# Diagonal products in four pieces, and another order of the node tiles, in a two-layer graph attention kernel

## The chip, the cores and the metric

The kernel runs on one core of a Trainium2 chip. The metric is the device time of one execution in microseconds (us); the time of a kernel is the median of its runs.

## The reference

The input is a graph with 10000 nodes of 768 float32 features and 170000 directed edges (`src`, `dst`, sorted by `dst`, one self-loop for each node). The reference adds a self-loop to every node again, which the kernel does by counting a node's own loop twice. What is computed, cut to what matters:

```python
def gat_conv(x, edge_index, W, a_src, a_dst, bias, heads, out_ch, concat):
    xl = (x @ W).reshape(n, heads, out_ch)
    e = leaky_relu(alpha_src[src] + alpha_dst[dst], 0.2)   # alpha = sum over channels of xl * a
    e = exp(e - segment_max(e, dst)[dst])
    alpha = e / (segment_sum(e, dst)[dst] + 1e-16)
    return segment_sum(xl[src] * alpha, dst) + bias        # 4 heads of 256, then 1 head of 768

h  = relu(layer_norm(gat_conv(x, W1 ...))) + (x @ Wr1 + br1)      # 1024 wide
h2 = layer_norm(gat_conv(h, W2 ...)) + (h @ Wr2 + br2)            # 768 wide
out = layernorm(x + h2)
```

## The kernel before, in words

**Preparation (0 to 888 us).** For each of 79 tiles of 128 nodes TensorE multiplies `x` by `W1` and the rows, with their attention terms, go to `table1` in HBM. Beside it VectorE and GpSimd sort the nodes by falling number of in-edges. From then on tile `t` holds the 128 nodes at places 128t to 128t+127 of that sorting, so tile 0 has the nodes with the most in-edges. The number of *slots* of a tile, the largest number of in-edges that its nodes may have, is fixed when the kernel is built (`slot_counts`): 41 for tile 0, then 27, 26, 25, 24, 24, 23, 23, 22 (four times), 21 (4), 20 (6), 19 (7), 18 (7), 17 (8), 16 (7), 15 (8), 14 (6), 13 (5), 12 (3), 11 (3), 10, 9 and 8; 1377 in all.

**The order of the tiles.** `TURNS` (L111) is the order in which both layers take the tiles. `paired` (L79) takes by turns one from the half with few in-edges and one from the half with many: it begins with 17, 17, 17, 17, 17, 18, 16, 18 slots, spreads to 11, 26, 9, 41, 10, 27, 11 in the middle, comes back to 18, 17, 18, 17, 17, and ends with the tile of 8.

**The ring.** A slot of a tile is one gathered row for each of its 128 nodes, one indirect DMA that GpSimd issues (L437). The rows go into a ring in SBUF, of 29 slots in layer 1 and of 41 in layer 2; slot number q+29 (q+41) is asked for once slot q has been read by all its readers (`Ring.fetch`). In layer 2 the first slot of a tile, its own rows, is a plain load on SyncE's queue (L465).

**Layer 1** (`ordered_layer1`). Each instruction stream is written out in the order of its engine, without a scheduler. For a tile: `weights_of` computes the attention weights `e` of all its slots (`logits`, L484; so all its slots must have landed), and for its first `on_pe(t)` slots (1 for tiles below 14 slots, 2 for 14 and 15, 3 for 16 and 17, 4 from 18) ScalarE writes, for each of the 4 heads, a 128x128 diagonal matrix with the weights (L735), by which TensorE multiplies the head's 256 columns of the gathered rows into the PSUM tile `acc` (`summed`, L741). The remaining slots are added into `acc` by VectorE: three in four have been multiplied by ScalarE (L521) and are added (L528), the fourth is multiplied and added head by head (L532). TensorE's other work for a tile does not depend on the slots: 14 transposes (L711), the product with `Wr1` (L184, 512 columns at a time), and the product with `W2` (L829). Its order is: diagonal products of tile t+1 behind the `W2` product of tile t-1, then the transposes and the `Wr1` product for tile t+1, then the `W2` product of tile t. The tile of 41 slots doesn't fit the ring and is taken in parts (`attend_parts`).

**Layer 2** (`ordered_layer2`). VectorE weighs and adds the first 512 of the 768 columns of every slot (L532). The last 256 columns are TensorE's: ScalarE writes one diagonal matrix for each slot (L939; five tiles of four matrices) and TensorE multiplies (L940) into the PSUM tile that holds the residual. The residual of a tile is `x` by an identity (L951) and `h` by `Wr2` (L954). TensorE takes the residual of tile t+2 after the diagonal products of tile t+1. The normalised rows are scattered to the output by GpSimd (L973).

A float32 product of TensorE appears in the profile as two passes, each a weight load (PEld) and a matmul (PE): 956 matrices of L735 make 1912 matmuls of L741, and 1377 of L939 make 2754 of L940.

Of the kernel before, what the change touches and what calls it, by code (L numbers as in the profile page):

```python
# [33 lines left out]
AX = mybir.AxisListType  # L34

P = 128
BANK = 512
BIG = 1.0e30
SLOPE = 0.2
# [6 lines left out]
G = 4  # L46
# [4 lines left out]
ON_PE2 = 512  # L51
# [4 lines left out]
def chunk_counts(n_edges):  # L56

    used = n_edges // P + 1
    return used, -(-used // P) * P + G


def slot_counts(n_nodes, n_edges):
# [7 lines left out]
    counts = []  # L70
    for t in range(-(-n_nodes // P)):
        room = t * P if t else 0.002
        k = next((k for k, m in enumerate(tails)
# [2 lines left out]
    return counts  # L76


def paired(n):  # L79

    last = n - 1
    half = last // 2
    many = list(range(half - 1, -1, -2))
    many += sorted(set(range(half)) - set(many))
    few = list(range(half, last, 2))
    few += sorted(set(range(half, last)) - set(few), reverse=True)
    turns = []
    for i in range(len(few)):
        turns += few[i:i + 1] + many[i:i + 1]
    return turns + [last]  # L90


@with_exitstack
def gnn_kernel(ctx, tc, x, x_cols, src, dst, src_col, dst_col, W1, a_src1, a_dst1, b1, g1, be1, Wr1, br1,
               W2, a_src2, a_dst2, b2, g2, be2, Wr2, br2, out, n_edges):
    nc = tc.nc
    N, D0 = out.shape
    H1, DH1 = a_src1.shape
    H2, DH2 = a_src2.shape
    C1, C2 = H1 * DH1, H2 * DH2  # L100


    R1, R2 = C1 + 2 * H1 + 1, C2 + 2 * H2
    NT = -(-N // P)
    NP = NT * P
    NCH = src_col.shape[1]
# [1 line left out]
    CAPS = slot_counts(N, n_edges)  # L108
    SLOTS = CAPS

    TURNS = paired(NT)  # L111
    FIRST, TOTAL = [0] * NT, 0
    for t in TURNS:
        FIRST[t], TOTAL = TOTAL, TOTAL + SLOTS[t]
# [50 lines left out]
    def transposed(pool, a, n, name):  # L165

        k = n // P
        aT = pool.tile([P, k, P], F32, name=name)
        for j in range(0, k, BANK // P):
            m = min(BANK // P, k - j)  # L170
            p = ps_tr.tile([P, BANK // P, P], F32, name="tr")
            for i in range(m):
# [4 lines left out]
    def product(aT, w, n, pool=None):  # L177

        k = w.shape[1]
        p = (pool or ps_big).tile([P, 2 * BANK], F32, name="big")  # L180
        for c in range(0, n, BANK):
            e = min(n, c + BANK)
            for j in range(k):
                nc.tensor.matmul(p[:, c:e], aT[:, j, :], w[:, j, c:e], start=(j == 0), stop=(j == k - 1))  # L184
        return p
# [298 lines left out]
    def logits(small, ring, lo, hi, ad, heads, c, top=None):  # L484


        n = hi - lo
        e = small.tile([P, ring.size, heads], F32, name="e")[:, :n]
        for a, b, rows in ring.parts(lo, hi):
            nc.vector.tensor_tensor(e[:, a - lo:b - lo], rows[:, :, c + heads:c + 2 * heads],  # L490
                                    ad[:, None, :].to_broadcast([P, b - a, heads]), op=OP.add)
        leaky(e, e)
        new = small.tile([P, heads], F32, name="new")
        nc.vector.reduce_max(new, e.rearrange("p k h -> p h k"), axis=AX.X)
        if top is not None:
            nc.vector.tensor_max(new, new, top)
        nc.vector.tensor_tensor(e, e, new[:, None, :].to_broadcast([P, n, heads]), op=OP.subtract)
        nc.scalar.activation(e, e, AF.Exp)  # L498
        for a, b, rows in ring.parts(lo, hi):
            if not ring.own:  # L500
                nc.vector.tensor_scalar(slots[:, a:b], rows[:, :, R1 - 1], -1.0, float(NP), op0=OP.mult, op1=OP.min)  # L501
                nc.vector.memset(rows[:, :, c + heads:], -BIG)
        return e, new

    def normalised(small, e, heads, t):

        doubled(e, t)
        total = small.tile([P, heads], F32, name="total")
        nc.vector.reduce_sum(total, e.rearrange("p k h -> p h k"), axis=AX.X)
        nc.vector.tensor_scalar(total, total, 1e-16, None, op0=OP.add)  # L510
        nc.vector.reciprocal(total, total)
        nc.vector.tensor_mul(e, e, total[:, None, :].to_broadcast([P, e.shape[1], heads]))  # L512

    def doubled(e, t):
        nc.vector.tensor_scalar(e[:, 0], e[:, 0], loops[:, TURNS[t]:TURNS[t] + 1], None, op0=OP.mult)

# [60 lines left out]
    def pieces(a, width):  # L577

        return [a[:, c:c + width] for c in range(0, a.shape[1], width)]
# [35 lines left out]
    with tc.tile_pool(name="w1", bufs=1) as w1p, tc.tile_pool(name="l1", bufs=2) as io, \  # L615
# [51 lines left out]
        for t in range(NT):  # L667
# [3 lines left out]
            for i, vec in enumerate((ad_b, as_b)):  # L671
                m = io.tile([P, C1], F32, name="scr")
                nc.vector.tensor_mul(m, p[:, :C1], vec)  # L673
                for h in range(H1):
                    s = slice(h * DH1, (h + 1) * DH1)
# [9 lines left out]

    SLOTS, FIRST = [SLOTS[t] for t in TURNS], [FIRST[t] for t in TURNS]

    def nodes(t):
        return order[:, TURNS[t]:TURNS[t] + 1]

    def ordered_layer1():
        with tc.tile_pool(name="b1", bufs=1) as pool, tc.tile_pool(name="small1", bufs=2) as small, \
# [3 lines left out]
            ring = Ring(pool, table1, R1, RING1, {})  # L696
# [34 lines left out]
            def summed(acc, diagonals, e, q, lo, hi, m):  # L731

                for k in range(lo, hi):
                    for i in range(H1):
                        nc.scalar.activation(diagonals[:, k * H1 + i, :], ident, AF.Copy,  # L735
                                             scale=e[:, k, i:i + 1])
                for k in range(lo, hi):
                    for i in range(H1):

                        c, d = i * DH1, (i + 1) * DH1  # L740
                        nc.tensor.matmul(acc[:, c:d], diagonals[:, k * H1 + i, :], ring.slot(q + k)[:, c:d],  # L741
                                         start=(k == 0 and c % BANK == 0),
                                         stop=(k == m - 1 and (d % BANK == 0 or d == C1)),
                                         skip_group_check=True)

            def weights_of(t):

# [13 lines left out]
            last = None  # L761
# [4 lines left out]
            def store(t):  # L766
# [5 lines left out]
                full = None  # L772
                nc.sync.dma_start(table2[TURNS[t] * P:(TURNS[t] + 1) * P, :], row)

# [5 lines left out]
            for t in range(NT + 1):  # L780
                live, events = t < NT, []
                n = SLOTS[t] if live else 0
# [13 lines left out]
                if whole:  # L796
                    e, acc = ready
# [49 lines left out]
                if live and not whole:  # L847
                    due(n)
                    sums, acc = (ps_acc.tile([P, 2 * BANK], F32, name="acc") for _ in range(2))
# [25 lines left out]
                last = None  # L875
                if live:
                    last = r, acc
            store(NT - 1)

    def ordered_layer2():  # L880
        nonlocal ps_big
        with tc.tile_pool(name="b2", bufs=1) as pool, tc.tile_pool(name="small2", bufs=2) as small, \
# [5 lines left out]
            parts = pieces(w2.rearrange("p k n -> p (k n)")[:, :6 * C1], C1)  # L888
            ring = Ring(pool, table2, R2, RING2, dict(zip(FIRST, TURNS)))

# [34 lines left out]
            def weights_of(t):  # L925


                n = SLOTS[t]
                ad = small.tile([P, H2], F32, name="ad")
                nc.vector.tensor_add(ad, ring.slot(FIRST[t])[:, C2:C2 + H2], lift)  # L930
                e, _ = logits(small, ring, FIRST[t], FIRST[t] + n, ad, H2, C2)
                yield e
                normalised(small, e, H2, t)
                to = rs[t][:, C2:2 * C2 - ON_PE2]
                nc.tensor.matmul(to, ones, b2_b[0:1, ON_PE2:], start=False, stop=False, skip_group_check=True)
                for k in range(n):
                    if k % G == 0:
                        diagonals = pool.tile([P, G, P], F32, name="diagonals", bufs=DIAGONALS)
                    nc.scalar.activation(diagonals[:, k % G, :], ident, AF.Copy, scale=e[:, k, :])  # L939
                    nc.tensor.matmul(to, diagonals[:, k % G, :], ring.slot(FIRST[t] + k)[:, ON_PE2:C2],  # L940
                                     start=False, stop=(k == n - 1), skip_group_check=True)
                yield

            def residual(t):
# [14 lines left out]
            def norms(t, h, r, means):  # L959

                stats = deviation(small, [a for m in means for a in pieces(m, C2 - ON_PE2)])
                yield
                scaled(h, means, stats, g2_b, be2_b)
                nc.vector.tensor_add(h, h, r[:, :C2])
                mean, inv = deviation(small, pieces(h, C2 // 2))
                yield
                nc.vector.reciprocal(inv, inv)
                less = small.tile([P, 1], F32, name="less")
                nc.vector.scalar_tensor_tensor(less, mean, -1.0, inv, op0=OP.mult, op1=OP.mult)
                o = pool.tile([P, C2], F32, name="out")  # L970
                nc.scalar.activation(o, h, AF.Identity, bias=less, scale=inv)
                yield
                nc.gpsimd.indirect_dma_start(  # L973
                    out=out, out_offset=bass.IndirectOffsetOnAxis(ap=nodes(t), axis=0),
                    in_=o, in_offset=None, bounds_check=N - 1, oob_is_err=False)

            assert C2 % BANK and C2 % BANK + C2 - ON_PE2 <= BANK
            q = product(brT, wr2, C2)
            rs = {0: residual(0)}
            last = iter(())  # L980
            ready = []
            assert whole(0)
            for t in range(NT):
                n = SLOTS[t]
# [3 lines left out]
                if not whole(t):  # L988
# [5 lines left out]
                    last = norms(t, h, rs[t], [h])  # L994
                else:
                    e = (ready or list(weights_of(t)))[0]
                    acc = ps_acc.tile([P, BANK], F32, name="acc")
# [24 lines left out]
                    last = norms(t, h, rs[t], [acc, rs[t][:, C2:2 * C2 - ON_PE2]])  # L1022
# [274 lines left out]
```

## Time and profile before

| | |
|---|---|
| median of 3 runs (lowest to highest) | 5709.45 us (5708.44 to 5711.98) |
| the profiled execution's own time | 5708.44 us |
| its span, first to last instruction | 5706.6 us |
| busy: TensorE / VectorE / GpSimd / ScalarE | 4919.0 / 4317.0 / 3222.9 / 3159.9 us |
| preparation, layer 1, layer 2 (first gather into the ring at 887.7, first residual near 3487) | 888, 2599, 2220 us |
| mean granted TensorE clock | 0.92 |

The busy time of TensorE counts a matmul from its start to a modelled end that lies behind the start of the next; the time from one start to the next is what a matmul takes in a stream. In a row of the timeline the first two numbers are the start and the length in us, then engine, line, operation, names, shapes and the number of instructions; in brackets stands the idle time before it and what ended it. "issue" there means that the engine waited for nothing that the profile shows.

### The profile page before, as it was taken

What the parts mean: (1) busy time and instruction counts of PE and PEld (TensorE: products, weight loads), DVE (VectorE), ACT (ScalarE), POOL (GpSimd) and SP (SyncE); (2) the same over time, 40 slices, a digit from 0 to 9 for tenths busy, and PEclk for the clock granted to TensorE, in tenths of its full rate; (3) what the DMA queues carried; (4) which work ended last, traced back from release to release, by engine and by line L of the source; (5) the groups of instructions that cost most, each with busy time, mean ns of one, the idle gap of its engine ahead of it and who ended that gap; (6) DMA issues with size and microseconds to landing.
All of it is one profiled execution on the core that took longest, in us unless ns stands there. A gap on an engine that the chain in (4) does not pass through costs nothing. (4 is left out here: it accounts for less than half of the span.)

```text
span 5706.6 us, 60022 instructions
## 1 busy us (share of the span) xinstructions
PE 4919.0 (86%) x15191; PEld 2904.7 (51%) x15191; DVE 4317.0 (76%) x7970; ACT 3159.9 (55%) x8255; POOL 3222.9 (56%) x3159
## 2 busy tenths in 40 slices
PE   8999996999998887788899998788888767888887
PEld 3444443555554544445555555455555444555554
DVE  5883345999888886888899994677877767777776
ACT  3434345888887775788888883333333333333332
POOL 3437355665565555555556653666666656666663
PEclk9999998999999888899999999888998888988988
DMA  4333637999999985899999986888888878888885
GB/s 154 120 103 86 91 94 293 357 362 351 334 345 320 326 304 213 304 332 337 326 348 349 363 315 228 301 292 313 304 307 315 287 249 295 308 311 308 311 301 171
DMA packets 474310, 1587.56 MB, mean 278 GB/s; under 512 B 119259, under 2 KB 123419, under 8 KB 473958
## 3 DMA queue, kind: packets, MB, share of 16 engines
q0 software_dynamic: 322384, 1282.77, 63.7%
q1 hardware_dynamic: 149520, 297.43, 15.7%
q10 hardware_dynamic: 2054, 3.42, 0.2%
q8 instruction: 128, 2.10, 0.1%
q14 instruction: 224, 1.84, 0.1%
HBM read 1431.80 MB, written 177.29 MB: 282 GB/s over the span
## 5 line engine op out<-in xcount | busy, mean ns | idle before, releaser
L437 POOL DMA_INDIRECT ring<-table,slots x2675 | 2643.7, 988 | 1823.7 <-issue 533.3
L532 DVE SCALAR_TENSOR_TENSOR acc<-ring,e,acc 128x512 f32<-128x512 f32 (+1 forms) x2530 | 1578.1, 624 | 163.1 <-PE acc L741 73.3
L521 ACT ACTIVATE ring<-ring,e 128x256 f32<-128x256 f32 x3284 | 1337.4, 508 | 0.0
L528 DVE TENSOR_TENSOR acc<-acc,ring 128x1024 f32<-128x1024 f32 x801 | 985.6, 1231 | 74.6 <-ACT ring L521 4.2
L954 PE MATMUL big<-wr,w 128*128 128x512 f32 (+1 forms) x2464 | 875.1, 501 | 134.2 <-issue 133.3
L940 PE MATMUL big<-ring,diagonals 128*128 128x256 f32 x2754 | 733.9, 423 | 237.0 <-issue 165.6
L184 PE MATMUL big<-wr,xT 128*128 128x512 f32 x1896 | 854.6, 608 | 0.2 <-ACT xT L712 0.2
L184 PE MATMUL big<-w,xT 128*128 128x512 f32 x1896 | 824.3, 596 | 26.6 <-DMA w<-in_W_dram 10.7
L829 PE MATMUL half<-w,hT 128*128 128x512 f32 (+1 forms) x2528 | 830.4, 486 | 0.0
L940 PEld LDWEIGHTS big<-ring,diagonals 128*128 128x128 f32 x2754 | 577.3, 213 | 392.2 <-issue 237.6
L954 PEld LDWEIGHTS big<-wr,w 128*128 128x128 f32 x2464 | 481.1, 196 | 497.9 <-issue 468.7
L939 ACT ACTIVATE diagonals<-ident,e 128x128 f32<-128x128 f32 x1377 | 421.9, 388 | 487.1 <-PE big L940 168.9
L829 PEld LDWEIGHTS half<-w,hT 128*128 128x128 f32 x2528 | 477.8, 189 | 372.8 <-issue 335.8
L741 PE MATMUL acc<-ring,diagonals 128*128 128x256 f32 x1912 | 471.4, 404 | 183.9 <-ACT diagonals L735 164.5
L184 PEld LDWEIGHTS big<-w,xT 128*128 128x128 f32 x1896 | 361.5, 191 | 485.0 <-issue 466.8
L184 PEld LDWEIGHTS big<-wr,xT 128*128 128x128 f32 x1896 | 366.7, 197 | 433.5 <-issue 432.9
L741 PEld LDWEIGHTS acc<-ring,diagonals 128*128 128x128 f32 x1912 | 381.8, 202 | 262.8 <-ACT diagonals L735 183.4
L589 ACT ACTIVATE sd<-mv,eps 128x1 f32<-128x1 f32 x237 | 69.7, 294 | 736.8 <-DVE mv L587 344.8
L673 DVE TENSOR_TENSOR scr<-big,ad_b 128x1024 f32<-128x1024 f32 x79 | 96.7, 1224 | 379.2 <-ACT row L670 355.3
L735 ACT ACTIVATE diagonals<-ident,e 128x128 f32<-128x128 f32 x956 | 292.7, 387 | 116.5 <-DVE e L512 89.6
L498 ACT ACT_TABLE_LOAD x154 | 197.6, 1283 | 276.7 <-DVE slots L501 69.4
L678 POOL TENSOR_TENSOR row<-row,none 128x1024 f32<-128x1024 f32 x79 | 187.1, 2369 | 264.5 <-ACT row L670 262.6
(174 smaller groups left out, 3906.9 us busy)
## 6 DMA issues: line engine op xcount, KB each, us to landing
ring<-table,slots POOLq DMA_INDIRECT x2675
table<-row SPq DMA_DIRECT2D x79, 516.0 KB
h_d<-hT SPq DMA_DIRECT2D x79, 512.0 KB
w<-h_d SPq DMA_DIRECT2D x77, 512.0 KB
table<-row SPq DMA_DIRECT2D x79, 385.0 KB
ring<-table SPq DMA_DIRECT2D x79, 385.0 KB
xT<-in_x_cols_dram SPq DMA_DIRECT2D x79, 384.0 KB
x_d<-xt SPq DMA_DIRECT2D x79, 384.0 KB
```

Source lines behind the costliest of these rows:

```text
L184: nc.tensor.matmul(p[:, c:e], aT[:, j, :], w[:, j, c:e], start=(j == 0), stop=(j == k - 1))
L437: nc.gpsimd.indirect_dma_start(out=to, out_offset=None, in_=table, in_offset=bass.IndirectOffsetOnAxis(ap=index, axis=0), **more)
L498: nc.scalar.activation(e, e, AF.Exp)
L521: nc.scalar.activation(row[:, s], row[:, s], AF.Copy, scale=e[:, h:h + 1])
L528: nc.vector.tensor_add(acc[:, :c], acc[:, :c], row[:, :c])
L532: nc.vector.scalar_tensor_tensor(acc[:, s], row[:, s], e[:, h:h + 1], (acc if first is None else first)[:, s], op0=OP.mult, op1=OP.add)
L735: nc.scalar.activation(diagonals[:, k * H1 + i, :], ident, AF.Copy, scale=e[:, k, i:i + 1])
L741: nc.tensor.matmul(acc[:, c:d], diagonals[:, k * H1 + i, :], ring.slot(q + k)[:, c:d], start=(k == 0 and c % BANK == 0), stop=(k == m - 1 ...
L829: nc.tensor.matmul(q, hT[:, j, :], w2[:, j, c:c + q.shape[1]], start=(j == 0), stop=(j == K1 - 1))
L939: nc.scalar.activation(diagonals[:, k % G, :], ident, AF.Copy, scale=e[:, k, :])
L940: nc.tensor.matmul(to, diagonals[:, k % G, :], ring.slot(FIRST[t] + k)[:, ON_PE2:C2], start=False, stop=(k == n - 1), skip_group_check=True)
L954: nc.tensor.matmul(r[:, c:d], hT[:, j, :], wr2[:, j, c:d], start=False, stop=(j == K1 - 1 and (d < C2 or not whole(t))), skip_group_check= ...
```

## The change

Two things change together. First, the order of the tiles: `paired` is gone, and `TURNS` becomes the tiles 78, 76, ... 2, 0 and then 1, 3, ... 77. The numbers of slots then rise 8, 10, 11, 12, 12, 13, ... 22, 23, 24, 26 to 41 and fall 27, 25, 24, 23, 22, ... 12, 11, 11, 9, so that neighbours differ by little. Second, each product with a diagonal matrix becomes four. In layer 1 a piece uses 32 columns of the matrix with all 128 rows and writes 32 partitions of `acc`; in layer 2 a piece uses one 32x32 block on the diagonal, with 32 partitions of the gathered rows. Each piece still streams 256 columns. The diagonal matrices and all else stay.

```diff
+QUAD = 32
-def paired(n):
-    ...
-    TURNS = paired(NT)
+    TURNS = list(range(NT - 1, -1, -2))
+    TURNS += sorted(set(range(NT)) - set(TURNS))
@@ summed, layer 1
-                        nc.tensor.matmul(acc[:, c:d], diagonals[:, k * H1 + i, :], ring.slot(q + k)[:, c:d],
-                                         start=(k == 0 and c % BANK == 0),
-                                         stop=(k == m - 1 and (d % BANK == 0 or d == C1)),
-                                         skip_group_check=True)
+                        for g in range(0, P, QUAD):
+                            nc.tensor.matmul(acc[g:g + QUAD, c:d], diagonals[:, k * H1 + i, g:g + QUAD],
+                                             ring.slot(q + k)[:, c:d], start=(k == 0 and c % BANK == 0),
+                                             stop=(k == m - 1 and (d % BANK == 0 or d == C1)),
+                                             skip_group_check=True)
@@ weights_of, layer 2
-                    nc.tensor.matmul(to, diagonals[:, k % G, :], ring.slot(FIRST[t] + k)[:, ON_PE2:C2],
-                                     start=False, stop=(k == n - 1), skip_group_check=True)
+                    for g in range(0, P, QUAD):
+                        s = slice(g, g + QUAD)
+                        nc.tensor.matmul(to[s], diagonals[s, k % G, s], ring.slot(FIRST[t] + k)[s, ON_PE2:C2],
+                                         start=False, stop=(k == n - 1), skip_group_check=True)
```

More of the change, by code (lines that the diff above doesn't have):

```diff
@@ L76, in slot_counts @@
     return counts
-def paired(n):
[L81 to L90, printed above, removed]
 @with_exitstack
```

## The prediction

> **What bounds the kernel now.** I read the page, then the busy times by stage, then the timeline of TensorE (PE) in both layers, then the waits. The page first: PE leads, but 86% is an average over three stages, and the last line is a chain of 1 us, so the stages have to be read one by one.
>
> ```profile
> PE 4919.0 (86%) x15191; PEld 2904.7 (51%) x15191; DVE 4317.0 (76%) x7970; ACT 3159.9 (55%) x8255; POOL 3222.9 (56%) x3159
> ```
>
> Layer 1, TensorE's timeline over one tile of 11 slots and the next, of 24:
>
> ```profile
> 2001.73 10.51 PE L829 MATMUL half<-w,hT 128*128 128x512 f32 x32
> 2012.08 7.08 PE L741 MATMUL acc<-ring,diagonals 128*128 128x256 f32 x32
> 2019.00 0.82 PE L711 MATMUL half<-ident,xt 128*128 128x128 f32 x6
> 2020.33 1.09 PE L711 MATMUL half<-ident,h 128*128 128x128 f32 x8 [0.51 <-ACT xT L712]
> 2021.26 10.46 PE L184 MATMUL big<-wr,xT 128*128 128x512 f32 x24
> 2031.56 10.51 PE L829 MATMUL half<-w,hT 128*128 128x512 f32 x32
> 2050.30 3.78 PE L741 MATMUL acc<-ring,diagonals 128*128 128x256 f32 x8 [8.23 <-ACT diagonals L735]
> ...
> 2070.88 4.46 PE L829 MATMUL half<-w,hT 128*128 128x512 f32 x10
> ```
>
> From one L829 to the next is a tile's interval. The first, 29.8 us, has no gap but 0.5: PE bounds the small tile, because its interval holds the 16 diagonal products (32 passes) of the large tile that follows. The second, 39.3 us, has PE idle; there VectorE, idle for 3 us only, bounds. Read so for all tiles, the mean interval by slots is 28.6 us (8 to 13 slots, 14 tiles), 29.8 (14 and 15; 14 tiles), 30.1 (16, 17; 15 tiles), 31.5 (18 to 21; 24 tiles) and 38.7 (22 to 27; 11 tiles); the tile of 41 takes 82.
>
> Layer 2, two tiles of 17 slots:
>
> ```profile
> 3574.61 5.43 PE L940 MATMUL big<-ring,diagonals 128*128 128x256 f32 x19
> 3581.26 0.38 PE L940 MATMUL big<-ring,diagonals 128*128 128x256 f32 x1 [1.23 <-issue]
> 3584.06 0.59 PE L940 MATMUL big<-ring,diagonals 128*128 128x256 f32 x1 [2.42 <-issue]
> ...
> 3598.77 2.72 PE L940 MATMUL big<-ring,diagonals 128*128 128x256 f32 x6 [0.82 <-issue]
> 3601.28 1.91 PE L951 MATMUL big<-w,ident 128*128 128x512 f32 x2
> ```
>
> ```profile
> PE big L940 <- issue: 165.6, 105, 3.1
> PE big L954 <- issue: 133.3, 114, 3.0
> POOL ring L437 <- PE big L940: 238.8, 132, 13.9
> ACT diagonals L939 <- PE big L940: 168.9, 61, 11.7
> ```
>
> PE runs fast, then crawls, its instructions 0.7 us or a multiple of that apart, until its residual comes; in the timeline this recurs in most tiles and adds up to some 410 us, none of it in layer 1. The last two rows tell who depends on PE: the gathers, whose slots it must free, and ScalarE. So layer 2 is PE's work plus its stalls.
>
> **The price of a piece.** A pass takes, from start to start, 0.429 us for 512 columns (L184), 0.215 for 256 (L940, L741), 0.109 for 128 (L711): time goes by the streamed columns, and the change leaves these at 256 while it makes 8 passes of 2. If the four pieces run side by side, a product stays at 0.43; if one waits for another, it takes 8 x 0.215 = 1.72. No row shows a piece. A price below 0.43 isn't excluded by any row, but nothing points to it. I take 0.86, by the row of the two passes: the second starts 0.215 behind the first, and pieces issued in order can overlap only the second pass of one with the first of the next, which leaves 4 x 0.215. The pace of issue gives the same: L711 makes one load and one matmul in 0.109, and 8 such pairs take 0.87.
>
> The Trainium skill (TensorE: Matmul & The Clock Gate, Packing small matmuls) has matmuls on different 32-wide tiles of the array start some 4 ns apart, which would leave a product near 0.43 and the sum at 5600 to 5750, as in the first two rivals. The same section has matmuls start and end strictly in program order, which with two passes to a piece would give 0.86 and 6185. The skill's page TensorEngine Tiling (Key Properties) adds that a change of tiling mode drains the array; no row here shows that.
>
> **Layer 1.** PE's part of an interval is 29.8 - 16 x 0.43 = 22.9 us and the next tile's products: 4, 8, 12 or 16. VectorE's part D is the measured interval where it bounds (28.9 at 18 slots, 32.4 at 20, 36.4 at 22, 43.8 at 27); below 17 slots I go down by 1.4 us a slot, the mean of three additions of 1.231 us and one of 4 x 0.489. In the new order neighbours are alike, so an interval is the larger of D and PE's part with the tile's own class. Means by class, as before:
>
> - 8 to 13 slots: D 23.9; PE 24.6 at 0.43, 26.3 at 0.86; interval 25.1 or 26.3.
> - 14, 15: D 27.1; PE 26.3, 29.8; interval 27.3 or 29.8.
> - 16, 17: D 28.8; PE 28.1, 33.2; interval 28.8 or 33.2.
> - 18 to 21: D 31.5; PE 29.8, 36.7; interval 31.7 or 36.7.
> - 22 to 27: D 38.8; PE 29.8, 36.7; interval 38.8 or 38.9.
>
> Times the tiles of a class, less the 2422 us measured for the same tiles: the order alone, at 0.43, is worth 2326 - 2422 = -96 us, since small tiles no longer carry 16 products. At 0.86 the sum is 2558, so +136. VectorE must also wait for the four first slots in `acc` before it adds its own: 16 products took 6.9 us and will take 13.8, behind e; the cover is its last three slots and the norm of the tile before, some 10 us. I put 0 to 5 us on each of 35 tiles with four such slots, 0 to +175, and take +50, for where PE bounds already the wait is inside. Layer 1: +186.
>
> **Layer 2.** PE's own work is 79 x 12.1 (residual and bias: 16 x 0.429 + 16 x 0.216 + 1.8) and 1377 products: 956 + 592 = 1548 us of 2220 before, 956 + 1184 = 2140 after. Of the other 672 us some 180 must stay (the 40 us to the first product, 65 at the end, the tile of 41). If all 672 stay, +592; if the stalls vanish under a slower PE, 2320 and +100. I take +300: the stalls come behind long unbroken trains of gathers, and a PE that frees slots later makes shorter ones. What is late next is ScalarE, whose twenty matrices are freed by L940, and behind its wait the standard deviations (L589), for which VectorE waits.
>
> The order in layer 2: tiles of 17 next to each other took 57.1 us for two (3583.5 to 3640.7, by VectorE's first addition of a tile), 21 and 13 slots 50.3 (4197.9 to 4248.2). So alike neighbours cost up to 3 us a tile over some 50 tiles, 0 to +150; under the slower PE I count it within the +300.
>
> **The rest.** Numbers of gathers (2675), of SyncE's loads and stores and of ScalarE's matrices (956 and 1377) don't change; each tile's go with it. The preparation is hidden as before under 888 us of products. Both layers begin with 8 slots in place of 17, nine gathers of 1.25 us less each before the first weights: up to -20, taken as -10. Sum on the execution's own 5708 (the median is 1 above): 5708 + 186 + 300 - 10 = 6184, say 6185. Its own bounds: 5708 + 136 + 100 - 20 = 5924 to 5708 + 136 + 175 + 592 = 6611.
>
> **The rivals.**
>
> - Pieces side by side, and the order pays: a product at 0.43, -96 in layer 1, nothing in layer 2, -10 at the starts: 5600, faster. For it: the classes above, and that no piece shares columns of the array. It decides below 0.48 us for a product, where 1377 x 0.05 and a little in layer 1 have used up the 96. Chance 0.17.
> - Pieces side by side, but alike neighbours cost layer 2 its full 150: 5708 - 96 + 150 - 10 = 5750. Chance 0.10, of which 0.03 within 0.2%, about what a measurement of this kernel can tell from no change.
> - The pieces don't overlap at all: 1.72. PE's intervals become 29.8 to 50.4, layer 1 +882 and up to +175; layer 2 956 + 1377 x 1.72 = 3324 and 180 to 672 of the rest, +1284 to +1776; some 8050. One layer alone so: 6900 or more. Chance 0.16.
> - The forecast, 0.57.
>
> So faster 0.17, same 0.03, slower 0.80. The range leaves out most of the third rival and little else: 5580 (a start of -20 and a little) to 6900.
>
> **What would show it.** L741 with 7648 and L940 with 11016 matmuls; the starts of eight passes of one product spread over 0.86 us (0.43 or 1.72 decide for a rival). In layer 1 intervals of 26, 30, 33 and 37 us by class without gaps on PE. In layer 2 fewer crawls, and more waiting of the gathers and of ScalarE on L940. Wrong would be PE idle in the intervals of 18 to 21 slots, or intervals in layer 2 as long as now.

## The result, and the profile after

The changed kernel takes 6065.67 us (median of 4 runs, 6047.57 to 6074.46); the kernel before, beside it, takes 5709.55 us. The ratio is 1.062, with a 95% interval of 1.059 to 1.064: slower. The profiled execution took 6067.82 us with a span of 6066.0.

Later runs went to other chips, each met in one session. On two of them (chips 6 and 13) the kernel before takes about 5380 us, on three (5, 12 and 0) about 5715, so every time below stands beside that of the kernel before on the same chip.

The page of the changed kernel, its busy line: the matmuls have grown from 15191 to 29189, PE's busy time by less than a tenth.

```profile
PE 5304.0 (87%) x29189; PEld 2703.1 (45%) x29189; DVE 4318.9 (71%) x7966; ACT 3174.3 (52%) x8255; POOL 3203.0 (53%) x3159
```

Layer 1, TensorE's timeline over one tile of the changed kernel (start and length in us, engine, line, operation, names, shapes, number; L818, L730 and L172 were L829, L741 and L184):

```profile
1086.22 10.51 PE L818 MATMUL half<-w,hT 128*128 128x512 f32 x32
1096.66 3.67 PE L730 MATMUL acc<-ring,diagonals 128*32 128x256 f32 x64
1100.27 0.88 PE L699 MATMUL half<-ident,xt 128*128 128x128 f32 x6
1101.65 1.09 PE L699 MATMUL half<-ident,h 128*128 128x128 f32 x8 [0.51 <-ACT xT L700]
1102.58 10.46 PE L172 MATMUL big<-wr,xT 128*128 128x512 f32 x24
1112.89 1.45 PE L818 MATMUL half<-w,hT 128*128 128x512 f32 x3
```

The 64 passes of L730 are eight products; from the first to the next instruction, at 1100.27, they take 3.61 us, 0.45 a product. The whole interval is 26.67 us without a gap but the 0.5 that was there before: 22.9 for the rest, and eight products at a little over 0.43.

Layer 2, TensorE's timeline of one tile of the changed kernel (L931, L945, L942 and L924 were L940, L954, L951 and L935):

```profile
4195.27 0.69 PE L924 MATMUL big<-b,ones 1*128 1x256 f32 x2
4195.89 4.36 PE L931 MATMUL big<-ring,diagonals 32*32 32x256 f32 x68
4201.05 1.10 PE L931 MATMUL big<-ring,diagonals 32*32 32x256 f32 x3 [0.80 <-issue]
4202.53 4.14 PE L931 MATMUL big<-ring,diagonals 32*32 32x256 f32 x32 [0.38 <-issue]
4207.03 0.62 PE L931 MATMUL big<-ring,diagonals 32*32 32x256 f32 x4 [0.36 <-issue]
4208.45 2.51 PE L931 MATMUL big<-ring,diagonals 32*32 32x256 f32 x5 [0.81 <-issue]
4211.30 1.08 PE L931 MATMUL big<-ring,diagonals 32*32 32x256 f32 x4 [0.33 <-issue]
```

Of the first 68 passes 64, eight products, start within 3.3 us (the last at 4199.17): 0.43 us a product. Then PE crawls: it waits for nothing that the profile shows ("issue"), and its instructions come in steps of 0.7 us; I call that a crawl, and one unbroken piece of it a stretch. The waits of the changed kernel (us in total, times, longest) hold the same:

```profile
PEld big L931 <- issue: 691.6, 912, 40.3
ACT diagonals L928 <- PE big L931: 454.0, 121, 16.4
POOL ring L425 <- PE big L931: 392.3, 118, 15.2
PE big L931 <- issue: 286.3, 353, 39.9
PE big L945 <- issue: 48.9, 39, 3.1
```

PE's issue waits at the diagonal products have grown from 165.6 to 286.3 us and shrunk at the residual (133.3 to 48.9), so the crawl has moved from the residual into the products. Most of its growth stands before the weight loads: their waits on issue at the products were 237.6 us before and are 691.6. The two that depend on PE, the gathers (238.8 to 392.3) and ScalarE (168.9 to 454.0), wait longer.

By stage, the sum of the tiles' intervals (layer 1 from L818 to L818, layer 2 from the first weighing of a tile on VectorE to the next tile's) goes from 2504 to 2498 us in layer 1 and from 2149 to 2533 in layer 2. The whole loss is in layer 2. To count the crawl, I take every stretch in which starts on PE (matmuls, weight loads and semaphore instructions together) follow by 0.7, 1.4, 2.1 or 2.8 us (to less than 25 ns) at least twice, with under 6 us between: 59 stretches and 421 us before, 71 and 773 us after, all in layer 2 (the changed kernel has one more, of 2.8 us, in layer 1, in the tile of 41).

### The profile page after: what moved, and what is told of

The parts are those of the page before. It is cut to its first block, busy times and chain, and to the rows that moved or that the text cites. A ratio compares the mean times of both kernels' runs of the same rounds, so it can differ in the third digit from the quotient of the medians.

```text
span 6066.0 us, 88315 instructions
## 1 busy us (share of the span) xinstructions
PE 5304.0 (87%) x29189; PEld 2703.1 (45%) x29189; DVE 4318.9 (71%) x7966; ACT 3174.3 (52%) x8255; POOL 3203.0 (53%) x3159
## 3 DMA queue, kind: packets, MB, share of 16 engines
q8 instruction: 237, 3.88, 0.3%
## 5 line engine op out<-in xcount | busy, mean ns | idle before, releaser
L520 DVE SCALAR_TENSOR_TENSOR acc<-ring,e,acc 128x512 f32<-128x512 f32 (+1 forms) x2530 | 1578.0, 624 | 164.2 <-PE acc L730 42.8
L931 PE MATMUL big<-ring,diagonals 32*32 32x256 f32 x11016 | 1091.1, 445 | 345.9 <-issue 286.3
L928 ACT ACTIVATE diagonals<-ident,e 128x128 f32<-128x128 f32 x1377 | 431.3, 389 | 1010.1 <-PE big L931 454.0
L945 PE MATMUL big<-wr,w 128*128 128x512 f32 (+1 forms) x2464 | 876.2, 507 | 49.5 <-issue 48.9
L931 PEld LDWEIGHTS big<-ring,diagonals 32*32 32x32 f32 x11016 | 515.4, 118 | 891.4 <-issue 691.6
L172 PE MATMUL big<-w,xT 128*128 128x512 f32 x1896 | 826.1, 597 | 26.9 <-DMA w<-in_W_dram 9.9
L172 PE MATMUL big<-wr,xT 128*128 128x512 f32 x1896 | 832.5, 595 | 0.2 <-issue 0.2
L818 PE MATMUL half<-w,hT 128*128 128x512 f32 (+1 forms) x2528 | 830.4, 486 | 0.0
L945 PEld LDWEIGHTS big<-wr,w 128*128 128x128 f32 x2464 | 492.5, 200 | 433.3 <-issue 401.8
L730 PE MATMUL acc<-ring,diagonals 128*32 128x256 f32 x7648 | 498.3, 411 | 209.3 <-ACT diagonals L723 188.0
L818 PEld LDWEIGHTS half<-w,hT 128*128 128x128 f32 x2528 | 477.8, 189 | 372.8 <-issue 332.0
L172 PEld LDWEIGHTS big<-w,xT 128*128 128x128 f32 x1896 | 362.2, 192 | 486.4 <-issue 468.2
L172 PEld LDWEIGHTS big<-wr,xT 128*128 128x128 f32 x1896 | 356.7, 192 | 419.7 <-issue 419.7
L573 DVE BATCH_NORM_STATS2 st<-big 128x6 f32<-128x256 f32 x79 | 33.8, 428 | 622.6 <-remote 363.5
L730 PEld LDWEIGHTS acc<-ring,diagonals 128*32 128x32 f32 x7648 | 264.7, 118 | 433.6 <-ACT diagonals L723 233.2
```

Of the source, the lines that this page charges most:

```text
L520: nc.vector.scalar_tensor_tensor(acc[:, s], row[:, s], e[:, h:h + 1], (acc if first is None else first)[:, s], op0=OP.mult, op1=OP.add)
L730: nc.tensor.matmul(acc[g:g + QUAD, c:d], diagonals[:, k * H1 + i, g:g + QUAD], ring.slot(q + k)[:, c:d], start=(k == 0 and c % BANK == 0), ...
L818: nc.tensor.matmul(q, hT[:, j, :], w2[:, j, c:c + q.shape[1]], start=(j == 0), stop=(j == K1 - 1))
L931: nc.tensor.matmul(to[s], diagonals[s, k % G, s], ring.slot(FIRST[t] + k)[s, ON_PE2:C2], start=False, stop=(k == n - 1), skip_group_check= ...
L945: nc.tensor.matmul(r[:, c:d], hT[:, j, :], wr2[:, j, c:d], start=False, stop=(j == K1 - 1 and (d < C2 or not whole(t))), skip_group_check= ...
```

## Experiments: the two parts, on a chip without crawls

Chip 6, kernel before 5382.67 us. The order alone:

```diff
-    TURNS = paired(NT)
+    TURNS = list(range(NT - 1, -1, -2))
+    TURNS += sorted(set(range(NT)) - set(TURNS))
```

> The new order with whole products. Theory I (the loss is the fours in layer 2, whose many instructions meet the stretches in which TensorE's instructions come 0.7 us apart): layer 1 near 2500 us as in the changed kernel, layer 2 at most 100 above the 2149 us between the first additions of the tiles, 5700 to 5800 in all. Theory II (the loss is the order, since neighbours alike press on the ring): layer 2 near the 2533 of the changed kernel, 6000 to 6070 in all.

Measured: 5353.39 us, ratio 0.995 (0.993 to 0.996). The four pieces alone, in both layers, that is the changed kernel with the order of before (the function `paired`, put back, isn't shown):

```diff
-    TURNS = list(range(NT - 1, -1, -2))
-    TURNS += sorted(set(range(NT)) - set(TURNS))
+    TURNS = paired(NT)
```

> The old order with fours in both layers. Theory I: layer 1 within 20 us of 2504 with the small tiles' intervals at 29.8 still, layer 2 250 to 400 above 2149, 5950 to 6100 in all. Theory II: within 30 us of 5710.

Measured: 5392.34 us, ratio 1.002 (1.001 to 1.003). And the kernel before with two pieces of 64x64 in layer 2 alone:

```diff
-                    nc.tensor.matmul(to, diagonals[:, k % G, :], ring.slot(FIRST[t] + k)[:, ON_PE2:C2],
+                    for g in range(0, P, 64):
+                        s = slice(g, g + 64)
+                        nc.tensor.matmul(to[s], diagonals[s, k % G, s], ring.slot(FIRST[t] + k)[s, ON_PE2:C2],
...
```

> The kernel before, and in layer 2 each product in two, by the 64x64 blocks on the diagonal: twice the instructions in place of four times. Theory I: a third of what the fours alone cost in layer 2, +80 to +140 us. Rival (any splitting of the array costs alike): as much as the fours.

Measured: 5380.91 us, ratio 1.000 (0.999 to 1.001). So here four pieces cost 0.2% and two nothing. The numbers in the three expectations were meant for a chip like the first, so the theories aren't told apart here, and the 80 to 140 us for two pieces didn't come. No trace on this chip has a crawl; layer 2 takes 1853, 1825 and 1828 us. TensorE's timeline of the order alone, on this chip:

```profile
4114.93 1.02 PE L952 MATMUL big<-w,ident 128*128 128x512 f32 x2
4115.78 7.03 PE L955 MATMUL big<-wr,w 128*128 128x512 f32 x16
4122.65 0.59 PE L952 MATMUL big<-w,ident 128*128 128x256 f32 x2
4123.08 3.62 PE L955 MATMUL big<-wr,w 128*128 128x256 f32 x16
4126.63 0.69 PE L936 MATMUL big<-b,ones 1*128 1x256 f32 x2
4131.85 11.67 PE L941 MATMUL big<-ring,diagonals 128*128 128x256 f32 x42 [4.53 <-ACT diagonals L940]
```

The residual runs through, and the only gap has a cause that the profile names: ScalarE's matrices.

A fourth run on this chip asked whether the number of instructions in itself costs: ahead of each whole product in layer 2 stand three products of one column by zeros, 32x32, which add nothing to the sum (the tile `zeros` is made ahead of the loop).

```diff
+                    for g in range(0, 96, 32):
+                        s = slice(g, g + 32)
+                        nc.tensor.matmul(to[s, 0:1], zeros[s, :], ring.slot(FIRST[t] + k)[s, ON_PE2:ON_PE2 + 1],
+                                         start=False, stop=False, skip_group_check=True)
```

> The kernel before, and in layer 2 three more products of one column with a matrix of zeros ahead of each diagonal product: as many instructions as the fours, but a whole diagonal product. Theory I, by the number of instructions: layer 2 as much longer as with the fours alone. A rival, that it is the 32x32 pieces in the array (or the changing between pieces and whole products, which happens here 17 times a tile in place of once): by the number of columns nothing, within 30 us of 5710; by the changing between forms, over 200 us more than the fours.

Measured: 5669.18 us, ratio 1.053 (1.052 to 1.055), layer 2 at 2105 us, again without a crawl. TensorE's timeline shows what it was:

```profile
4206.29 0.23 PE L944 MATMUL big<-ring,zeros 32*32 32x1 f32 x6
4206.45 0.70 PE L946 MATMUL big<-ring,diagonals 128*128 128x256 f32 x2
4207.08 0.23 PE L944 MATMUL big<-ring,zeros 32*32 32x1 f32 x6
4207.24 0.70 PE L946 MATMUL big<-ring,diagonals 128*128 128x256 f32 x2
```

A product now comes every 0.79 us (4206.29 to 4207.08) in place of 0.43. The 0.36 is paid for the three tiny products and for going from the 32x32 form to the whole form and back; no run separates the two. That is the last case of the expectation, over 200 us more than the fours (277). So this run told nothing of the number of instructions; it gave a bound for a change of form, which the changed kernel makes only twice for each tile of layer 2. The Trainium skill (TensorEngine Tiling, Key Properties) says that changing the tiling mode drains TensorE; the 0.36 us fit that, and are the most that a pair of changes can cost here.

## Experiments: the two parts, on chips with crawls

Chip 5, kernel before 5716.33 us. The changed kernel once more, and the order alone once more:

> The changed kernel, unaltered. Where the kernel before takes some 5380 us and has no stretches with TensorE's instructions 0.7 us apart: by theory I (order -30, fours +10 where there are none of these stretches) 5340 to 5400, within 1% of before. Where the kernel before takes some 5710 us and has them: 6065 again. Rival (order and fours together cost what neither costs alone): 6% above before in either case.

> The new order with whole products once more. Where the kernel before has the stretches (some 5710 us): theory I 5700 to 5800, with the rest of the way to 6065 due to the fours; theory II (the order makes the stretches longer) 5950 to 6070. Where it has none: 5350 as in the first run of this kernel.

Measured: 6077.55 us, 1.062 (1.060 to 1.065), with 770 us of crawls; and 5665.02 us, 0.991 (0.988 to 0.993), with 402 us in 61 stretches. Layer 2 takes 2534 and 2145 us. So the order is a gain here too, and the four pieces cost 412 us on top of it. A third look at the changed kernel came on chip 12 (kernel before 5706.78):

> The changed kernel, unchanged, once more, for the chip that it lands on. Theory A (the loss of 6.2% is nothing but the steps of 0.7 us that the larger number of TensorE instructions brings, on chips where such steps occur at all): where the kernel before takes about 5380 and its trace shows no such steps, the changed kernel takes 5340 to 5375, a ratio of 0.992 to 0.999, layer 2 about 1850 us; where the kernel before takes about 5715, it takes about 6075 again, 1.062, with some 770 us of steps. Rival B (four pieces cost layer 2 some 5 us for each tile on any chip): 1.05 to 1.065 on both.

Measured: 6057.05 us, 1.061 (1.059 to 1.063), 751 us of crawls. It came to no chip without crawls, so its time there wasn't measured; from the order alone (0.995), the pieces alone (1.002) and two pieces in layer 2 with the new order (0.996, below) I estimate about 0.996.

## Experiments: what makes TensorE crawl

In the kernel before, a stretch begins late in an unbroken train of gathers. TensorE's and GpSimd's timelines of the kernel before:

```profile
3892.91 8.45 PE L940 MATMUL big<-ring,diagonals 128*128 128x256 f32 x38 [0.35 <-issue]
3901.20 1.02 PE L951 MATMUL big<-w,ident 128*128 128x512 f32 x2
3902.06 7.03 PE L954 MATMUL big<-wr,w 128*128 128x512 f32 x16
3908.92 0.59 PE L951 MATMUL big<-w,ident 128*128 128x256 f32 x2
3909.36 2.97 PE L954 MATMUL big<-wr,w 128*128 128x256 f32 x13
3913.66 0.38 PE L954 MATMUL big<-wr,w 128*128 128x256 f32 x1 [1.34 <-issue]
```

```profile
3893.86 0.94 POOL L437 DMA_INDIRECT ring<-table,slots  x1 [3.08 <-DVE acc L532]
3895.11 0.94 POOL L437 DMA_INDIRECT ring<-table,slots  x1 [0.30 <-DVE total L510]
...
3917.06 0.95 POOL L437 DMA_INDIRECT ring<-table,slots  x1 [0.30 <-issue]
3922.90 0.95 POOL L437 DMA_INDIRECT ring<-table,slots  x1 [4.89 <-PE big L940]
```

The gathers come every 1.25 us from 3893.86 to 3917.06. From the first of them PE makes about 67 matmuls (some 34 of the 38, then 2, 16, 2 and 13), then crawls until a few us behind the last gather. In the changed kernel it was 68 passes from the tile's first product; the first gather started a little later, at 4196.83, and from it there are 48. Counts that near each other at 18 us and at 4 us are what led to theory A: with a train of gathers TensorE lives on the instructions that it has in hand, and gets new ones only in steps of 0.7 us. Two pieces in place of four, with the rest of the change kept, are the dose between. The first run fell on a chip without crawls (chip 13, kernel before 5374.06):

```diff
-                    for g in range(0, P, QUAD):
-                        s = slice(g, g + QUAD)
+                    for g in range(0, P, 64):
+                        s = slice(g, g + 64)
```

> The changed kernel, but layer 2's products in two pieces by the 64x64 blocks on the diagonal in place of four by the 32x32 blocks: 8 instructions on TensorE for each product (weight loads and matmuls) where the changed kernel has 16 and the kernel before 4. Theory A (TensorE has some 130 instructions in hand when a train of gathers on GpSimd begins, gets almost no new ones while it lasts, and then starts one every 0.7 us): the 130 last for 16 products, about 7 us, in place of 8 products, 3.5 us, and 32 products, 18 us; so the steps of 0.7 us add up to some 600 us, between the 402 of the new order with whole products and the 770 of the changed kernel, and the time is about 5860 (5760 to 5980) where the kernel before takes 5715. Rival B (the cost hangs on pieces as such, by array form): as the changed kernel, 6075, or, if only the 32x32 form is dear, as the new order alone, 5665. On a chip where the kernel before takes 5383 and no steps of 0.7 us are seen, both give about 5355.

Measured: 5354.21 us, 0.996 (0.995 to 0.998), no crawl. The second fell on chip 0 (kernel before 5721.42):

> The new order, fours in layer 1, and layer 2's products in two pieces of 64x64, once more: 8 instructions for each product on TensorE. Where the kernel before takes about 5380, 5354 as on the first such chip. Where it takes about 5715: theory A (some 130 instructions in hand at the start of a train of gathers, then almost none) puts the steps of 0.7 us between those of whole products (402 us) and those of fours (770 us), some 600 us, their starts some 8 us into a train, and the time at 5760 to 5980; if the form of the pieces decided, it would be 5665 (only the 32x32 form is dear) or 6060 (any pieces are).

Measured: 5746.35 us, 1.004 (1.002 to 1.006), 457 us of crawls in 73 stretches. TensorE's timeline:

```profile
4196.77 7.12 PE L931 MATMUL big<-ring,diagonals 64*64 64x256 f32 x63
4204.87 0.40 PE L931 MATMUL big<-ring,diagonals 64*64 64x256 f32 x1 [0.98 <-issue]
4206.28 0.41 PE L931 MATMUL big<-ring,diagonals 64*64 64x256 f32 x1 [1.01 <-issue]
4207.70 0.67 PE L931 MATMUL big<-ring,diagonals 64*64 64x256 f32 x1 [1.02 <-issue]
4209.12 2.72 PE L931 MATMUL big<-ring,diagonals 64*64 64x256 f32 x10 [0.74 <-issue]
```

Again some 63 matmuls, now 7 us, then steps. All four side by side, on chips with crawls; the starts are medians over the stretches, counted from the first indirect DMA of the train, and the instructions are weight loads, matmuls and semaphore instructions:

| kernel | instructions per product, layer 2 | stretch starts after: us, PE instructions | crawls | layer 2 |
|---|---|---|---|---|
| before | 4 | 18.4, 131 | 421 us | 2149 us |
| new order, whole products | 4 | 17.8, 125 | 402 us | 2145 us |
| new order, two pieces | 8 | 8.6, 113 | 457 us | 2207 us |
| the change, four pieces | 16 | 3.5, 96 | 773 us | 2533 us |

The time to the stretch falls five-fold, the number of instructions by a quarter. The time in the run of two pieces lies between whole products and four, as theory A had it and neither case by form did, though just below its own range from 5760; its crawls, put at some 600 us, came to 457. So the rise is steep only from two pieces to four, and the theory has the order but not the sizes.

The trains taken one by one bear it out. For each I count PE's instructions from its first gather to its last (a train has no pause above 0.5 us). In layer 2 of the kernel before, a stretch starts within a train, or within 1 us behind its last gather, in 39 of the 47 trains with 120 instructions or more and in 10 of the 78 with fewer; in the changed kernel, in 54 of the 67 trains with 90 or more and in 10 of the 203 with fewer. Layer 1 has gathers too, but its trains are short: over 100 instructions fall within 1 of its 470 trains before and within 3 of 512 in the changed kernel, and its one stretch lies in the fullest of these, with 411. It begins there only after some 350 instructions, so the count isn't a fixed one.

What if GpSimd doesn't gather in layer 2? In the next kernel the four pieces stay, and the same number of bytes per slot comes by plain loads on SyncE's queue, of 128 rows that lie together and so not of the right neighbours:

```diff
-                elif q < self.size or self.own:
+                elif self.own:
+                    nc.sync.dma_start(self.slot(q), self.table[q % NT * P:(q % NT + 1) * P, :])
+                elif q < self.size:
```

> The changed kernel with its fours, but layer 2's neighbours come by plain loads that SyncE issues (128 rows of the table that lie together, so the wrong neighbours), not by GpSimd's gathers: the same bytes, no gather on GpSimd. Theory A: no steps of 0.7 us are left in layer 2, though a product still has 16 instructions; layer 2 takes 1900 to 2200 us in place of 2533 and the whole 5450 to 5700 where the kernel before takes 5715. Rival C (any heavy traffic keeps instructions from TensorE): the steps stay at some 770 us, and the time at 6000 to 6100. On a chip without the steps (before at 5383) both give 5300 to 5450.

> The changed kernel with layer 2's neighbours brought by plain loads from SyncE (128 rows that lie together, the wrong neighbours) in place of GpSimd's gathers, once more. Where the kernel before takes about 5380: 5220 as on the first chip. Where it takes about 5715: by theory A (TensorE's instructions are held up by trains of gathers on GpSimd) no steps of 0.7 us in layer 2 and 5220 to 5350, some 750 us less than the changed kernel; by rival C (by any heavy traffic) the steps stay near 770 us and the time near 5950 to 6100.

Measured: on chip 13, 5219.96 us, 0.971 (0.970 to 0.973); on chip 12, 5250.23 us, 0.920 (0.918 to 0.922), where the changed kernel took 6057. Neither has a crawl in layer 2. TensorE's timeline on chip 12, and then its groups of instructions (number | busy us, mean ns | idle time before them and what ended it):

```profile
4190.41 12.23 PE L933 MATMUL big<-ring,diagonals 32*32 32x256 f32 x176 [3.25 <-ACT diagonals L930]
4202.56 1.12 PE L944 MATMUL big<-w,ident 128*128 128x512 f32 x2
4203.53 7.03 PE L947 MATMUL big<-wr,w 128*128 128x512 f32 x16
```

```profile
L933 PE MATMUL big<-ring,diagonals 32*32 32x256 f32 x11016 | 636.0, 385 | 85.3 <-ACT diagonals L930 85.2
```

176 passes in one run, and of the changed kernel's 345.9 us of idle time before the diagonal products, 286.3 of it on issue, 85 are left, none on issue. With the same 11016 passes, layer 2 takes 1725 us in place of 2528. Many instructions alone don't make PE crawl, nor do 385 KB a slot: it takes the gathers. A gather differs from a plain load in the engine that issues it, in its queue and in its scattered rows; which of these counts wasn't tried. On the chip without crawls the same edit gave 134 us over two pieces with gathers (layer 2 at 1724 against 1845), so there the gathers' own pace is a limit.

A pause in the trains was to let PE be refilled. The kernel has the new order and whole products, and beside these lines only the scratch tile:

```diff
+                        if k == n // 2:
+                            for _ in range(8):
+                                nc.gpsimd.memset(idle, 0.0)
```

> The new order with whole products, and half-way through each layer-2 tile GpSimd writes zeros to a scratch tile eight times, about 4 us in all, so that no train of its gathers is longer than some 10. Theory A: TensorE is refilled in the pause and again at the tile's end; the steps of 0.7 us fall from 402 us to under 150, and the time from 5665 to 5400-5580 where the kernel before takes 5715. If the pause is too short to refill (stretches ended 3.5 us after the last gather), the steps stay and the time is 5665 to 5750. Rival D (the steps come at a point of each tile whatever GpSimd does): 400 us of steps, and 5665 to 5980 with the pauses on top. On a chip without the steps: 5353 plus 0 to 100, since gathers have little slack.

Measured on chip 13: 5649.32 us, 1.051 (1.049 to 1.053); layer 2 at 2144 us where the order alone had 1853. GpSimd's group in this run:

```profile
L1018 POOL MEMSET idle<- 128x512 f32 x632 | 332.8, 527 | 31.9
```

333 us of pauses cost 296 us: GpSimd has next to no slack in layer 2. My 0 to 100 was wrong, and the trains can't be broken in this way for free. Whether pauses stop the crawl wasn't seen, since this chip has none.

The fastest version that computes the reference is the new order with whole products, 0.995 and 0.991 of the kernel before, or, on a chip without crawls, equally with two pieces in layer 2 (0.996).

## Why the prediction was right in its sign and wrong in its reason

The time fell inside the range, 119 us below the 6185; but the sum was 5708 + 186 + 300 - 10, and what came, in the profiled execution, was 5708 - 6 + 384 - 19 (the last for all outside the two layers' intervals). The sum was 192 us too high in layer 1 and 84 too low in layer 2; that the second takes back a part of the first is luck. The class of 16 and 17 slots goes into the prediction's sums with 14 tiles, not with the 15 that it names, since 79 starts make 78 intervals; that changes nothing else.

- **The price of a piece** is the step that failed first. I took 0.86 us a product, reasoning that pieces issued in order overlap only the second pass of one with the first of the next. In the trace four pieces start within 0.07 us, and the next four 0.15 us behind (layer 1: 2177.864, .894, .916, .930; then 2178.079, .112, .135, .149); a product takes 0.43. All first-pass and second-pass matmuls of one product share the time of two whole passes. My second argument, the pace of L711's loads, failed too: the four loads of layer 1 overlap. The Trainium skill (TensorE: Matmul & The Clock Gate, Packing small matmuls) had the start of tiles 4 ns apart and 0.43 as I read it, which I set aside; the median step here is 7 ns. It also has weight loads overlap matmuls in flight only where the row groups differ; the loads of L730 use all rows, take 108 ns each and start 14 to 30 ns apart, beside matmuls that the profile shows for 378 ns, so this trace disagrees.
- **Layer 1, +186** became -6. At 0.43 the classes were reckoned at 25.1, 27.3, 28.8, 31.7 and 38.8 us; they measure 24.3, 27.6, 29.2, 33.2 and 41.9, and the tile of 41 takes 99.8 in place of 82. The small tiles gain as reckoned. The large ones lose it again, and that is the order's doing: with whole products (the order alone, chip 5) they have 32.7, 41.9 and 99.4. I had let D, VectorE's part, stand as measured between small neighbours. Why the interval is longer between large ones wasn't tried; a limit that the prediction didn't price is in the profile. From 1700 to 1900 us, among tiles of 19 and 20 slots, the changed kernel's DMA engines are busy 0.96 of the time at 355 GB/s and VectorE 0.88; in the kernel before, with small tiles between, the DMA share is 0.92 at 330 GB/s (1600 to 2000 us). The prediction's own sign of error, PE idle in the intervals of 18 to 21 slots, is there: 33.2 us, of which PE's part is 29.8.
- **VectorE's wait for `acc`, +50**: it fell, from 73.3 us to 42.8 (`acc` of L532 and L520 on the diagonal products, in the waits).
- **Layer 2, +300** (+384 measured). The size is near, the working wrong on both counts. PE's own work, put at +592, didn't grow. And the stalls, which I let half vanish because a slower PE makes shorter trains, grew by 352. The trains did get shorter (without a pause of more than 0.5 us: 125 trains of a median of 13 gathers before, 270 of 4 after), and the stalls grew all the same. I had seen that they follow unbroken trains of gathers, but took the trains' length for the cause; the experiments point to how many instructions PE spends within a train, which the change multiplies. That the size came near 300 is luck. "Fewer crawls, and more waiting of the gathers and of ScalarE" came half true.
- **The order in layer 2, 0 to +150**: 2149 to 2145 on chips with crawls. Without, 1825 or 1828 (old order, with four or two pieces) and 1853 (new order, whole products): at most some 30 us of cost.
- **The rivals.** "Pieces side by side, and the order pays" had the mechanism, and on a chip without crawls it would, by the estimate of 0.996, have had the sign, with about 20 us in place of 106. What I didn't price, there or in the forecast, was the number of instructions as such: 58,000 loads and matmuls where there were 30,000, beside a symptom, waits on issue, that was in my own rows.

## What to carry to other kernels

Where a profile shows TensorE waiting on "issue" beside trains of indirect gathers, count its instructions before splitting a matmul: the pieces here ran side by side and took PE no longer, but each costs a load and a matmul for every pass. Try fewer pieces first (on chips with crawls two cost some 80 us over the order alone, four 412), and judge a symptom like this on more than one chip, for it may be absent on the next. Orders that put like tiles together help where one engine bounds, but check the class whose slack came from its neighbours.

## What the runs showed of the hardware

- The same kernel took 5374 to 5383 us on two chips and 5707 to 5721 on three, 6% apart. Where one kernel was traced on both kinds, nearly all of it lies in layer 2, where the crawl is: 292 of 309 us with the new order and whole products, 361 of 393 with two pieces. On the chips without, trains of up to 209 gathers at 1.25 us (order alone, chip 6) leave PE undisturbed. What sets a chip, or its session, apart stays open.
- That PE's supply of instructions runs dry is an inference, from the near-constant count and from the run without gathers. The DMA rows show a part of the supply. A queue of the kind "instruction" moves 16 KB packets in step with PE's instructions, one for some 254 of them, 128 before (2.10 MB) and 237 (3.88 MB) in the changed kernel. PE's stretches don't wait for these packets: in layer 2 a packet takes 0.97 us in the kernel before and 0.99 without crawls (order alone, chip 6), and of the 59 stretches before only 2 have a packet start within them, of the changed kernel's 71 only 27; the others end without one. If the supply runs dry, it is behind these packets. No row shows that, nor why a step is 0.7 us.
- The granted clock over layer 2 (from the first tile's weighing to the last's) is 0.82 in the changed kernel, 0.88 with two pieces, and 0.88 too in the run with pauses, which has no crawl but PE waiting for ScalarE's matrices; with the new order alone, without crawls, it is 0.93. So the lower clock goes with PE's waits, of whatever cause, and isn't special to the crawl. What it costs wasn't separated.
- GpSimd issues one gather in 1.25 us, and layer 2 has 1298 of them (1377 slots less 79 own rows): 1622 us of the 1853 that it takes in the new order on a chip without crawls.
